# Four cross-attention layers on one Trainium2 core: normalisations and a rotation mask on another engine, scores copied out of PSUM by the instruction that takes their maximum, a fifth share of banks, new ranks

## The chip, the core and the metric

The kernel runs on one core of a Trainium2 chip. A core has a matrix engine (TensorE, PE in the profile, with PEld for its weight loads) and three engines for elementwise work: VectorE (DVE), ScalarE (ACT) and GpSimd (POOL). SyncE (SP) issues the transfers. Matrix products land in PSUM, eight banks of 128 partitions by 512 words; everything else lives in SBUF. Each engine works through its own queue of instructions in order and waits at semaphores for the others. The metric is the device time of one execution in microseconds; the time before is the median of five executions.

## The reference

Sixteen batches of 100 query rows (width 256) pass through four cross-attention layers with 16 heads each, over the same 361 context rows. All is fp32. Cut to what matters:

```python
# L0: heads of 16, layer norm on both sides, then a feed-forward block
qn, kn = layer_norm(x), layer_norm(ctx)
a = softmax(Q(qn) @ K(kn).T / 4); x = x + (a @ V(kn)) @ wo + bo
x = x + gelu(layer_norm(x) @ w1 + b1) @ w2 + b2
# L1: heads of 64, root-mean-square norm on the queries, plain context, no scaling of scores
x = x + (softmax(Q(rms(x)) @ K(ctx).T) @ V(ctx)) @ wo
# L2: heads of 64, rotary embedding on queries and keys, mask over the context
s = rope(Q(x)) @ rope(K(ctx)).T / 8
s = where(mask, s, -1e9)
x = layer_norm(x + (softmax(s) @ V(ctx)) @ Wo) * gamma + beta
# L3: as L0 without the feed-forward block, its own weights
x = x + (softmax(Q(layer_norm(x)) @ K(layer_norm(ctx)).T / 4) @ V(layer_norm(ctx))) @ Wo + bo
```

A softmax here is: the maximum of a row, the exponential of the difference with its sum, a division by the sum.

## The kernel before

**Planned work.** The kernel does not emit instructions as it describes them. `Plan.add` records some 9,000 pieces of work, each with the engines that may do it, a cost, and the buffers that it reads, writes and takes. `Plan.order` (lines 212 to 306) then puts all pieces of all sixteen batches in one order by a simulation of its own: among the pieces whose inputs are done, it takes the one that could start earliest, and among equals the one with the lowest rank. A rank (line 220) is the batch's number times `ORDER["lag"]`, less the length of the chain behind the piece, plus an offset by batch and one for each place in a batch (`ORDER["place"]`, a table of 561 numbers). The same order holds for every engine's queue, so the planner decides what stands behind what. It also chooses between ScalarE and VectorE where a piece names both (copies out of PSUM, biases).

**Tilings.** TensorE works in several tilings: products of the projections and of the weighted values on 32 columns at a time (`col32`), transposes and the scores of heads of 64 on 64 rows (`row64`), the scores of heads of 16 on 32 rows (`row32`). A change of tiling between two pieces costs time; the planner knows it as `Plan.CHANGE` (line 152) and delays such a change by `keep`, `run` and `pull`.

**One unit of attention** (`Attention.unit`, line 817) is four heads. Its scores (L831) take one PSUM bank per head, [100, 361]; `ps_sc`, `SCORE_BANKS = 4` shares, keep the number of banks that hold scores to four of the eight. `exponential` (line 868) then works head by head: in L2 VectorE caps the scores with the mask in place in PSUM (L876); VectorE takes the negated maximum from PSUM (L879); ScalarE reads PSUM and writes the exponential to SBUF with its sum (L882). VectorE inverts the sums of a pair of heads (L854), GpSimd multiplies them in (L861, `divide`), TensorE transposes the pair (L915), ScalarE or VectorE copies the transposes out (L606, L608), and TensorE multiplies with the values (L725). A head's bank is given back when its last reader is done, here the exponential.

**Normalisation.** `inv_root` takes statistics on VectorE (L620 to L627) and a power on GpSimd (L630). `normalize` (L642), the context's three parts (L1271), and L1's scaling (L1286) run on VectorE, from SBUF to SBUF, and TensorE transposes the results (L666, L753). The feed-forward block's result is transposed back to rows at L708 (`rows_of`), from what L1021 adds up.

**Mask.** `make_cap` (L1297) turns the mask bytes into a cap on the scores, on VectorE, for the 100 query partitions. `make_rot` (L1301, L1302) multiplies the rotary tables with the mask bytes on VectorE, so that masked keys become zero. `rotated` (line 769) shuffles pairs on VectorE (L780), multiplies by the sine on GpSimd (L784), by the cosine on VectorE (L787) and adds on GpSimd (L792).

All four layers' instructions pass through the helper lines L606 and L608 (copies), L666, L708, L753, L915 (transposes), L725 (products on columns) and L831 (scores).

Of the kernel before, what the change touches and what calls it, by code (L numbers as in the profile page):

```python
# [19 lines left out]
SK = 361  # L20
# [6 lines left out]
SCORE_BANKS = 4  # L27
# [4 lines left out]
for _name, _w in (  # L32
# [23 lines left out]
    "lag": 78500, "pull": 0.15, "window": 0,  # L56
    "keep": {None: 260, "row64": 220, "row32": 1340, "col64": 2740, "col32": 2110},
    "run": {None: 2810, "row64": 13010, "row32": 14900, "col64": 44290, "col32": 780},
    "batch": (-373500, -1500, 0, 0, 0, 0, 0, 0, 0, 0, 0, 0, 0, 0, -500, -101500),
    "place": [  # L60
        100 * k for k in (
        -195, -25, -956, -1835, -2152, -1031, -1024, -1302, -380, -1684, -1378, -1056, -2143,
        -3503, -2138, -785, -673, -898, 960, -3089, -1622, -888, -1707, -1518, -697, -2594,
        -1339, 95, -552, 834, -1404, -127, -1261, 691, -1769, -3240, -2203, -1157, -1048, 28,
        -1351, -688, -920, -3022, -2221, -2884, -2570, -893, -1744, -2029, -1358, -1963, -574,
        -1155, 17, -756, -2041, -1521, -115, 97, -2134, -4053, -2742, -2111, -2818, -3840,
        -3124, -2876, -1724, -2610, -1441, -3183, -2751, -1243, -1194, -1293, -1145, -686,
        -1119, -1340, -1567, -372, -1031, -924, -2292, -848, 330, 279, 565, -1967, 77, 555, 176,
        -1213, 1890, -682, -1361, -1145, -1613, -2407, -1524, -908, -122, -819, 363, 658, -473,
        671, -312, 275, 803, -56, 224, -1068, -948, 39, -279, 909, 806, 1495, -2344, -641, -365,  # L70
        -2056, 268, 288, 371, -1596, 97, -666, 268, -99, -912, -1342, 664, 971, -162, 644,
        -2607, -1012, -1477, -1806, 110, -1358, -539, -1658, -1535, -477, -899, -135, -1284,
        -619, 912, -401, -85, 320, 1932, 139, -495, -184, 373, -167, -1736, -2576, -440, -217,
        2246, 1243, 167, -139, 817, -1953, -1661, -831, -1697, -332, -1702, -1275, 647, -1595,
        -338, -311, 1148, -1881, -2507, 316, 60, -1823, -8, -1720, -1704, -2198, 50, -2294, 227,
        -718, -333, 1067, 939, 1526, 2811, 212, 1614, -551, 1129, 1032, -489, -2063, 1566, 391,
        952, 203, 611, -129, 132, -78, -1417, -567, 299, 448, 34, -1821, -2597, -2358, -1036,
        -2125, -2751, -2686, -3064, -2566, -4629, -3070, -2280, -1071, -1526, -1652, -1425,
        -1803, -508, -1150, -3650, -1097, -629, -517, 152, -837, -182, -1836, -3200, -737,
        -2498, -1874, 832, -530, -447, -2212, -811, -888, -361, 1315, 84, -1531, 1226, -1587,  # L80
        325, -31, 611, -703, -1882, -102, 203, 100, -832, -220, -996, 1738, 1396, -461, -29,
        -186, 425, 1942, 563, -1378, 733, -6, 2603, 957, 1730, 475, 1401, 1309, 1431, 1393,
        1046, 1305, 985, 1138, 1299, 1081, 573, 1031, 3224, 1048, 1840, 1548, -36, 2079, 1728,
        -1588, -474, -1298, 34, -1814, -781, 1055, 812, 1176, -13, -223, 927, -121, -918, -1891,
        542, -375, 108, 550, -762, -322, 2130, 778, 1512, 1173, 2043, -384, 987, 383, -1008,
        1609, 1373, 1568, 2086, 3318, 3261, 1652, 1329, 652, 1387, 1281, 1633, -27, -308, 884,
        802, 727, -1112, -1621, -2396, -2191, -1331, -1775, 125, 665, -848, -538, 626, -628,
        1211, -537, 607, 1132, 273, -239, 28, 243, 305, -968, -2434, -2636, -2999, -2756, -2813,
        -2412, -2656, -2757, -996, -1431, -1348, -1738, -815, -1208, -2176, -2606, -696, 149,
        1101, -1463, -246, 554, 851, 43, 447, -61, -1392, 1231, 2636, 1100, 200, 331, 1125,  # L90
        1372, 2256, 1020, 986, 332, -1869, -1024, 963, -1748, -457, -2009, -1127, -1766, -3067,
        -2131, -3307, -3273, -4501, -3681, -3221, -2173, -2533, -2964, -5483, -5952, -4641,
        -4415, -2515, -2844, -3131, -3493, -139, 1783, 1636, 111, -1738, -520, -2114, -467,
        -962, 670, -259, -911, 2485, -2308, -501, -251, -2029, 352, -2107, -2183, -1114, 430,
        541, 75, 191, 448, 1236, 131, -2089, -699, -515, -2298, -775, 1387, 926, 2000, 1287,
        1330, 136, -1539, -1198, -419, -1538, -1836, 213, -574, 658, 632, 33, 915, -2280, 1047,
        -440, 1179, 1894, -793, 84, 1260, -1193, -1769, -318, -140, 261, -262, -542, -17, 555,
        -472, -262, 648, -1141, -836, -1855, -208, -131, 359, 1186, 589, 1619, -405, -1818,
        -2228, -556, -264, 755, 859, 1634, 1016, 1947, 706, 874, 137, -104, 716, -1426, -878,
        -1224, -621, -2026, 618, 901, 695, -388, -1702, -260, -2743, -2366, -3079, -1700, -4642,  # L100
        -1450, -1770, -2191, -1929, -1118, -755, -1793, -2871, -5035,
# [48 lines left out]
class Plan:  # L150

    CHANGE = {"row64": 175, "row32": 204, "col64": 172, "col32": 160, None: 190}
# [157 lines left out]
def tile_xattn_layers(  # L310
# [301 lines left out]
    def inv_root(srcs, eps, name, square=False):  # L612
# [4 lines left out]
        def stats(_):  # L617
            for j, (b, f, n) in enumerate(srcs):
                a = mv.ap
                nc.vector.bn_stats(a[:n, j, 2:8], f(b.ap))  # L620
                nc.vector.bn_aggr(a[:n, j, 0:2], a[:n, j, 2:8])
                if square:
                    nc.vector.scalar_tensor_tensor(
                        a[:n, j, 1:2], a[:n, j, 0:1], a[:n, j, 0:1], a[:n, j, 1:2],
                        ALU.mult, ALU.add,
                    )
            nc.vector.tensor_scalar(mv.ap[:, :k, 2], mv.ap[:, :k, 1], eps, None, ALU.add)  # L627

        def power(_):
# [4 lines left out]
        plan.add(  # L634
            on_dve(550, k), stats, reads=[b for b, _, _ in srcs], writes=[mv]
        )
        plan.add(on_pool(550), power, reads=[mv], writes=[mv])
        return mv

    def normalize(mv, dst, src, dst_f, src_f, j, n):  # L640
        def fn(_):
            nc.vector.tensor_scalar(  # L642
                dst_f(dst.ap), src_f(src.ap), mv.ap[:n, j, 0:1], mv.ap[:n, j, 3:4],
                ALU.subtract, ALU.mult,
            )

        plan.add(on_dve(E), fn, reads=[mv, src], writes=[dst])
# [4 lines left out]
    def queries_T(src, p, name, cls="xT", affine=None):  # L652
# [20 lines left out]
        for i, (q0, q1) in enumerate(parts):  # L673
# [6 lines left out]
            for c in range(2):  # L680

                def scaled(eng, i=i, c=c, q0=q0, q1=q1):
# [8 lines left out]
                    on_act(q1 - q0 + 100) + on_dve(q1 - q0 + 60), scaled,  # L691
# [107 lines left out]
    class Attention:  # L799
# [17 lines left out]
        def unit(self, i):  # L817
# [9 lines left out]
            def scores(_):  # L827
# [11 lines left out]
                on_pe((half, 4 * len(groups))), scores, reads=[self.q, *keys],  # L839
# [28 lines left out]
        def exponential(self, bank, share, sums, j, h, probs):  # L868
            neg_max = plan.buf("two", f"mx_{self.name}_{h}")
            prob = probs[h] = plan.buf("prob", f"prob_{self.name}_{h}")  # L870

            def s():
                return bank.ap[:S, :SK]
# [512 lines left out]
```

## Time and profile before

| what | value |
|---|---|
| median of 5 executions | 1969.51 us (1965.54 to 1971.88) |
| the profiled execution's own time | 1965.42 us |
| its span | 1963.5 us |
| granted TensorE clock, mean | 0.995 |
| TensorE busy with matmuls | 1914.3 us, 97% |
| GpSimd: divide (L861), 1024 instructions | 576.7 us, 579 ns each |
| ScalarE: exponential (L882), 1024 | 566.7 us, 565 ns each, and 204 ns each to read the accumulator |
| VectorE: normalisation of rows (L642), 48 | 38.4 us, 800 ns each |
| VectorE: normalisation of the context (L1271), 48 | 31.0 us, 651 ns each |
| VectorE: rotation mask (L1301 and L1302), 16 each | 931 and 1581 ns each |

How to read it: a line of a group names the source line, the engine, the operation, what it writes and reads with shapes, the count, the busy time and the mean of one in ns, and behind the bar the idle time of that engine just before these instructions and who ended it. In the timeline a line begins with its start and its length in us. A line of the waits reads "who waited for whom: us in total, times, longest". Matmuls are pipelined, so their lengths overlap; the distance from one start to the next tells more.

### The profile page before, as it was taken

How to read it: one execution, taken by the hardware profiler on the slowest of the kernel's cores; microseconds unless marked ns; L12 is line 12 of the kernel's file. 1: busy time of each engine (PE TensorE's matmuls, PEld its weight loads, DVE VectorE, ACT ScalarE, POOL GpSimd, SP SyncE). 2: the span in 40 equal slices, each digit the busy share in tenths (PEclk: the TensorE clock that was granted, in tenths of full speed). 3: DMA queues.
4: the chain of work that ended last, by engine and by line, in shares of the span. 5: the costliest groups of instructions: out<-in, count | busy, mean ns of one | idle time of the engine just before them, and what ended most of it. 6: DMA issues, size and time to landing. Idle time of an engine off the chain costs nothing.

```text
span 1963.5 us, 99209 instructions
## 1 busy us (share of the span) xinstructions
PE 1914.3 (97%) x43881; PEld 1266.9 (65%) x43881; DVE 1387.9 (71%) x3802; ACT 1134.2 (58%) x3398; POOL 958.0 (49%) x1522
## 2 busy tenths in 40 slices
PE   8999999999999999999999999999999999999997
PEld 4766575666766657666576666757566676665765
DVE  5656777767777677777767777677776777766676
ACT  4545555565556656566565665655556555664645
POOL 4354545544455453545445455454554445544544
PEclk9999999999999999999999999999999999999998
DMA  7000000000000000000000000000000000000000
GB/s 300 3 3 14 5 12 7 3 14 5 14 5 3 14 5 14 6 11 6 5 14 5 12 8 3 14 5 12 7 4 14 5 14 5 4 14 5 3 3 7
DMA packets 14726, 29.91 MB, mean 15 GB/s; under 512 B 3362, under 2 KB 12376, under 8 KB 12888
## 3 DMA queue, kind: packets, MB, share of 16 engines
q1 hardware_dynamic: 14296, 23.56, 3.7%
q8 instruction: 345, 5.65, 1.2%
q14 instruction: 85, 0.70, 0.1%
HBM read 21.92 MB, written 1.64 MB: 12 GB/s over the span
## 4 chain that ended last, share of the span: by engine, by line
PE 82%; DVE 11%; POOL 3%; issue 1%; ACT 1%; DMA 1%; SPq 0%; ACTq 0%; POOLq 0%; DVEq 0%
PE ps L725 58%; PE ps L831 12%; PE ps L915 10%; POOL prob L861 2%; DVE two L879 2%; DVE ps L876 1%; DVE rot L1302 1%; POOL sw L784 1%; DVE mv L620 1%; DVE ctxr L1271 1%; DMA slab<-slabs_dram 1%; PE ps L666 1%; DVE sw L780 1%; ACT prob L882 1%; DVE z L642 1%
## 5 line engine op out<-in xcount | busy, mean ns | idle before, releaser
L861 POOL TENSOR_SCALAR prob<-prob,two 100x361 f32<-100x361 f32 x1024 | 576.7, 579 | 729.7 <-DVE two L854 693.7
L882 ACT ACTIVATE prob<-ps,two 100x361 f32<-100x361 f32 x1024 | 566.7, 565 | 288.8 <-DVE two L879 260.9
L879 DVE TENSOR_REDUCE two<-ps 100x1 f32<-100x361 f32 x1024 | 486.4, 524 | 163.5 <-PE ps L831 162.2
L725 PE MATMUL ps<-slab,cT 128*32 128x512 f32 (+1 forms) x3072 | 363.4, 595 | 0.8 <-DMA slab<-slabs_dram 0.8
L725 PE MATMUL ps<-cT,slab 128*32 128x361 f32 x4096 | 357.0, 468 | 1.5 <-DMA slab<-slabs_dram 1.2
L831 PE MATMUL ps<-kT,qT 32*100 32x181 f32 (+3 forms) x4096 | 301.0, 328 | 0.3 <-DVE qT L1087 0.3
L606 ACT COPY pT<-ps 128x384 f32<-128x384 f32 (+1 forms) x522 | 232.2, 497 | 96.0 <-PE ps L915 63.5
L831 PEld LDWEIGHTS ps<-kT,qT 32*100 32x100 f32 (+1 forms) x4096 | 229.8, 165 | 77.1 <-issue 38.9
L915 PEld LDWEIGHTS ps<-ident,prob 64*128 64x128 f32 (+1 forms) x6144 | 214.6, 139 | 89.8 <-POOL prob L861 43.7
L915 PE MATMUL ps<-ident,prob 64*128 64x64 f32 (+1 forms) x6144 | 238.5, 226 | 11.7 <-POOL prob L861 11.6
L882 ACT ACTIVATION_READ_ACCUMULATOR prob<-ps,two 100x1 f32 x1024 | 208.9, 204 | 0.0
L725 PEld LDWEIGHTS ps<-cT,slab 128*32 128x32 f32 x4096 | 123.9, 109 | 116.4 <-issue 101.8
L725 PEld LDWEIGHTS ps<-slab,cT 128*32 128x32 f32 (+1 forms) x3072 | 88.1, 108 | 152.0 <-issue 136.4
L608 DVE COPY pT<-ps 128x384 f32<-128x384 f32 (+1 forms) x246 | 134.1, 570 | 63.8 <-PE ps L915 51.2
L784 POOL TENSOR_TENSOR sw<-sw,rot 128x361 f32<-128x361 f32 x128 | 105.6, 826 | 141.0 <-PE ps L725 66.7
L606 ACT COPY v<-ps 105x512 f32<-105x512 f32 (+1 forms) x145 | 84.9, 586 | 144.6 <-PE ps L725 144.5
L725 PE MATMUL ps<-pT,v 128*32 128x100 f32 (+1 forms) x6144 | 160.1, 251 | 2.1 <-DVE pT L608 1.2
L725 PEld LDWEIGHTS ps<-pT,v 128*32 128x32 f32 (+1 forms) x6144 | 138.4, 110 | 36.0 <-issue 27.2
L876 DVE TENSOR_TENSOR ps<-ps,cap 100x361 f32<-100x361 f32 x256 | 125.0, 532 | 22.5 <-PE ps L831 21.7
L725 PEld LDWEIGHTS ps<-xT,slab 128*32 128x32 f32 x5120 | 115.0, 111 | 20.5 <-issue 15.4
L725 PE MATMUL ps<-xT,slab 128*32 128x100 f32 x5120 | 125.2, 251 | 1.8 <-issue 1.4
L792 POOL TENSOR_TENSOR kT<-kT,sw 128x361 f32<-128x361 f32 x128 | 122.3, 957 | 3.9
(101 smaller groups left out, 2152.0 us busy)
## 6 DMA issues: line engine op xcount, KB each, us to landing
slab<-slabs_dram SPq DMA_DIRECT2D x11, 1024.0 KB
ctxr<-ctx_dram SPq DMA_DIRECT2D x16, 256.0 KB
ctxr<-ctx_dram SPq DMA_DIRECT2D x16, 105.0 KB
x<-x_dram SPq DMA_DIRECT2D x16, 100.0 KB
out_dram<-x SPq DMA_DIRECT2D x16, 100.0 KB
slab<-slabs_dram SPq DMA_DIRECT2D x2, 512.0 KB
mask<-mask_dram SPq DMA_DIRECT2D x16, 45.1 KB
rows<-rowvecs_dram SPq DMA_DIRECT2D x1, 640.0 KB
```

The source lines that it names most:

```text
L606: nc.scalar.copy(dst(), src())
L608: nc.vector.tensor_copy(dst(), src())
L620: nc.vector.bn_stats(a[:n, j, 2:8], f(b.ap))
L725: nc.tensor.matmul(out_f(at + t, at + t1), lhsT=lhsT[:, t:t1], rhs=rhs, start=start, stop=stop, tile_position=(0, at + t),)
L784: nc.gpsimd.tensor_tensor(a, a, wide(sin()), ALU.mult)
L792: nc.gpsimd.tensor_tensor(dst_f(dst.ap), dst_f(dst.ap), sw.ap[:, :n], ALU.add)
L831: nc.tensor.matmul(banks[h].ap[:S, k0:k1], lhsT=self.q_of(h), rhs=self.k_of(h)[:, k0:k1], start=(k0 == 0), stop=(k1 == SK), skip_group_che ...
L861: nc.gpsimd.tensor_scalar(p.ap[:S, :SK], p.ap[:S, :SK], rsum.ap[:S, j : j + 1], 1.0, ALU.mult, ALU.mult,)
L876: nc.vector.tensor_tensor(s(), s(), self.cap.ap[:S, :], ALU.min)
L879: nc.vector.tensor_reduce(neg_max.ap[:S, 0:1], s(), AX.X, ALU.max, negate=True)
L882: nc.scalar.activation(prob.ap[:S, :SK], s(), AF.Exp, bias=neg_max.ap[:S, 0:1], accum_out=sums.ap[:S, j : j + 1],)
L915: nc.tensor.transpose(out[:, c, :], probs[h].ap[q0:q1, c * KP : (c + 1) * KP], ident[q0:q1, q0:q1],)
```

## The change

The change moves work between engines, changes what frees a bank of scores, and sets new constants for the planner:

- `normalize` runs on GpSimd, as (x + (-mean)) x root; `inv_root` negates the mean for it, in one more VectorE instruction. The context's three parts and L1's scaling go the same way.
- The rotation mask is made on GpSimd, by clipping the cap to 0..1 and multiplying the two tables with that; the cap is now made on all 128 partitions.
- Unmasked heads (L0, L1, L3): one VectorE instruction reads the scores from PSUM, writes their negatives to SBUF and accumulates the minimum, which is the negated maximum; the exponential then reads SBUF with scale -1. Masked heads (L2): the cap's minimum is written to SBUF, and maximum and exponential read it there. The bank and its share are given back after VectorE's reading.
- Five shares for banks of scores in place of four; other costs for a number of pieces; other `CHANGE` values; another `ORDER`.

```diff
-SCORE_BANKS = 4
+SCORE_BANKS = 5
 ORDER = {
-    "lag": 78500, "pull": 0.15, "window": 0,
-    "keep": {None: 260, "row64": 220, "row32": 1340, "col64": 2740, "col32": 2110},
-    "run": {None: 2810, "row64": 13010, "row32": 14900, "col64": 44290, "col32": 780},
-    "batch": (-373500, -1500, 0, 0, 0, 0, 0, 0, 0, 0, 0, 0, 0, 0, -500, -101500),
+    "lag": 262500, "pull": 1.05, "window": 0,
+    "keep": {None: 4710, "row64": 360, "row32": 180, "col64": 5940, "col32": 2180},
+    "run": {None: 0, "row64": 28190, "row32": 38220, "col64": 62800, "col32": 390},
+    "batch": (-548000, -33500, 0, 0, 0, 0, 0, 0, 0, 0, 0, 0, 0, 0, 14000, -395500),
...
-    CHANGE = {"row64": 175, "row32": 204, "col64": 172, "col32": 160, None: 190}
+    CHANGE = {"row64": 170, "row32": 191, "col32": 141, None: 190}
...
             nc.vector.tensor_scalar(mv.ap[:, :k, 2], mv.ap[:, :k, 1], eps, None, ALU.add)
+            nc.vector.tensor_scalar(mv.ap[:, :k, 4], mv.ap[:, :k, 0], -1.0, None, ALU.mult)
...
     def normalize(mv, dst, src, dst_f, src_f, j, n):
         def fn(_):
-            nc.vector.tensor_scalar(
-                dst_f(dst.ap), src_f(src.ap), mv.ap[:n, j, 0:1], mv.ap[:n, j, 3:4],
-                ALU.subtract, ALU.mult,
+            nc.gpsimd.tensor_scalar(
+                dst_f(dst.ap), src_f(src.ap), mv.ap[:n, j, 4:5], mv.ap[:n, j, 3:4],
+                ALU.add, ALU.mult,
             )
-        plan.add(on_dve(E), fn, reads=[mv, src], writes=[dst])
+        plan.add(on_pool(395), fn, reads=[mv, src], writes=[dst])
...
             def mask_off(_):
-                nc.vector.tensor_tensor(s(), s(), self.cap.ap[:S, :], ALU.min)
+                nc.vector.tensor_tensor(p(), bank.ap[:S, :SK], self.cap.ap[:S, :], ALU.min)
             def maximum(_):
-                nc.vector.tensor_reduce(neg_max.ap[:S, 0:1], s(), AX.X, ALU.max, negate=True)
+                nc.vector.tensor_reduce(neg_max.ap[:S, 0:1], p(), AX.X, ALU.max, negate=True)
+            def negated(_):
+                nc.vector.tensor_scalar(
+                    p(), bank.ap[:S, :SK], -1.0, None, ALU.mult, ALU.min,
+                    accum_out=neg_max.ap[:S, 0:1],
+                )
             def exp(_):
                 nc.scalar.activation(
-                    prob.ap[:S, :SK], s(), AF.Exp, bias=neg_max.ap[:S, 0:1],
+                    p(), p(), AF.Exp, bias=neg_max.ap[:S, 0:1], scale=1.0 if masked else -1.0,
                     accum_out=sums.ap[:S, j : j + 1],
                 )
-            if self.cap is not None:
-                plan.add(on_dve(SK), mask_off, reads=[bank, self.cap], writes=[bank])
-            plan.add(on_dve(SK), maximum, reads=[bank], writes=[neg_max])
+            if masked:
+                plan.add(on_dve(SK), mask_off, reads=[bank, share, self.cap], writes=[prob])
+                plan.add(on_dve(SK), maximum, reads=[prob], writes=[neg_max])
+            else:
+                plan.add(on_dve(SK + 70), negated, reads=[bank, share], writes=[prob, neg_max])
             plan.add(
-                [("ACT", 538.0, 660.0)], exp, reads=[bank, share, neg_max], writes=[prob, sums]
+                [("ACT", 538.0, 660.0)], exp, reads=[prob, neg_max], writes=[prob, sums]
             )
...
-            nc.vector.tensor_scalar(z.ap, xt.ap, mv.ap[:S, 0, 3:4], None, ALU.mult)
+            nc.gpsimd.tensor_scalar(z.ap, xt.ap, mv.ap[:S, 0, 3:4], 1.0, ALU.mult, ALU.mult)
...
         def make_rot(_):
-            nc.vector.tensor_tensor(rot.ap[:, 0, :], cos_k, mu.ap, ALU.mult)
-            nc.vector.tensor_tensor(rot.ap[:, 1, :], sin_k, mu.ap, ALU.mult)
+            on = rot.ap[:, 0, :]
+            nc.gpsimd.tensor_scalar(on, cap.ap, 1.0, 0.0, ALU.min, ALU.max)
+            nc.gpsimd.tensor_tensor(rot.ap[:, 1, :], sin_k, on, ALU.mult)
+            nc.gpsimd.tensor_tensor(on, cos_k, on, ALU.mult)
```

The table `ORDER["place"]` is new throughout.

## The prediction

> **What bounds the kernel now.** I read the busy shares first, then the chain of work that ended last, then the groups, and last the waits and the timeline around the places where TensorE stood still. All durations are of the one profiled execution (span 1963.5 us, its time 1965.4 us).
>
> ```profile
> PE 1914.3 (97%) x43881; PEld 1266.9 (65%) x43881; DVE 1387.9 (71%) x3802; ACT 1134.2 (58%) x3398; POOL 958.0 (49%) x1522
> PE 82%; DVE 11%; POOL 3%; issue 1%; ACT 1%; DMA 1%; SPq 0%; ACTq 0%; POOLq 0%; DVEq 0%
> ```
>
> TensorE is the bound, and the change leaves its 43,881 matmuls as they are. So the time can only change by what stands between the matmuls: changes of the array's tiling, and waits. I measured both as the distance from the first matmul of one planned piece (1,973 in all) to the first of the next, and took the median of a piece followed by one of its own tiling as its price.
>
> ```profile
> 1050.53 1.05 PE L725 MATMUL ps<-slab,oT 128*32 128x256 f32 x16
> 1051.51 0.59 PE L753 MATMUL ps<-ident,ctxr 64*128 64x64 f32 x12
> ...
> 1052.77 1.06 PE L725 MATMUL ps<-slab,zT 128*32 128x256 f32 x16
> 1053.66 1.89 PE L725 MATMUL ps<-slab,cT 128*32 128x512 f32 x16
> ```
>
> Sixteen matmuls of one size take 0.98 us before transposes (another tiling; 1050.53 to 1051.51) and 0.89 before a piece of their own. Medians over all records: such a piece 863 ns and 977; the wide value piece 1717 and 1831; key projection 1214 and 1328; transposes 372 and 491. A tiling change costs 93 to 119 ns. The account closes: first matmul at 6.0, pieces 1795.2, 752 tiling changes 81.0, 94 waits over 100 ns 63.3, jitter 13.0, which makes 1958.4, where the last piece starts; 5.1 us follow.
>
> Of the 63.3, 11.0 lie in the first 100 us (weights, folding) and 21.5 in the last 60 (two batches left, little to fill in). In the middle the order repeats with each batch, and 26 us are three places, 14 times each: 0.64 us ahead of the transposes of L0's normalised rows, 0.51 ahead of those of the feed-forward result, and right after it 0.70 ahead of L2's probabilities (1.86 per batch). The waits name their releasers, some 14 to 16 times each where the place has the line for itself:
>
> ```profile
> PEld ps L708 <- ACT prob L882: 14.5, 14, 1.1
> PEld ps L666 <- DVE z L642: 13.5, 16, 1.6
> ```
>
> And the timeline shows why they are late:
>
> ```profile
> 1054.09 1.18 DVE L1271 TENSOR_SCALAR ctxr<-ctxr,mv 128x256 f32<-128x256 f32 x1
> ...
> 1056.01 1.11 DVE L642 TENSOR_SCALAR z<-x,mv 100x256 f32<-100x256 f32 x1
> ...
> 1057.17 0.33 PE L666 MATMUL ps<-ident,z 64*128 64x64 f32 x4 [0.58 <-DVE z L642]
> ```
>
> ```profile
> 1105.77 1.82 DVE L1302 TENSOR_TENSOR rot<-cst,mask 128x361 f32<-128x361 f32 x1 [1.79 <-POOL sw L784]
> ...
> 1107.51 0.97 DVE L876 TENSOR_TENSOR ps<-ps,cap 100x361 f32<-100x361 f32 x2
> ...
> 1112.24 2.20 POOL L861 TENSOR_SCALAR prob<-prob,two 100x361 f32<-100x361 f32 x4 [4.21 <-DVE two L854]
> ...
> 1112.55 0.32 PE L708 MATMUL ps<-ident,rT 64*100 64x64 f32 x4 [0.45 <-ACT prob L882]
> ```
>
> Normalisations and the rotation mask run on VectorE from SBUF to SBUF while GpSimd is at work there too, and take two to three times what such a shape costs elsewhere:
>
> ```profile
> L642 DVE TENSOR_SCALAR z<-x,mv 100x256 f32<-100x256 f32 x48 | 38.4, 800 | 26.3 <-POOL mv L630 26.3
> L1302 DVE TENSOR_TENSOR rot<-cst,mask 128x361 f32<-128x361 f32 x16 | 25.3, 1581 | 23.3 <-POOL sw L784 23.3
> L1313 DVE TENSOR_SCALAR x<-x,mv 100x256 f32<-100x256 f32 x16 | 7.0, 435 | 9.4 <-POOL mv L630 9.4
> L879 DVE TENSOR_REDUCE two<-ps 100x1 f32<-100x361 f32 x1024 | 486.4, 524 | 163.5 <-PE ps L831 162.2
> ```
>
> **The change part by part.**
>
> *Normalisations and rotation mask to GpSimd.* VectorE loses 48 x 800 + 48 x 651 (L1271) + 16 x 345 (L1286) + 16 x (931 + 1581) = 115 us and gains 96 negations at 172 (L627) = 16.5. GpSimd gains 112 one-input instructions; the divide, 361 wide, takes 579 (L861), by proportion 411 at 256, and the one 256-wide row 497 (L536), so I take 0.45 each, 50 us, and 16 masks of one one-input and two two-input instructions (579 + 2 x 826, L784) = 36 us: 958 becomes 1044, 53%. The first place (0.64) loses the two slow instructions of the timeline; the chain gets a negation of 0.17 and loses 0.35 of normalisation and a hop between engines. The third place (0.70) loses the 1.82 us ahead of L876. What may now be late is the normalisation itself, queued on GpSimd behind up to four divides (2.2 us, as at 1112.24).
>
> The Trainium skill speaks against this part: its GPSIMD Engine Reference, section "Engine selection", sends elementwise work to VectorE and calls GpSimd about twice as slow with two inputs. The rows here say the opposite for this place: VectorE took 800 and 1581 where GpSimd takes 579 and 826. By the rule this part would lose time on the chain; by the rows it takes away the waits above.
>
> *Scores leave PSUM with their maximum.* For 768 unmasked heads a TENSOR_SCALAR with an accumulated minimum takes the place of a 524 ns reduce. No row shows VectorE accumulating. Lower end: 524, since a plain PSUM copy of this width takes 529 (L608) and no row is faster. Upper end: 587 (L1052, same shape, PSUM to SBUF) plus 204, what ScalarE pays to read its accumulator (L882), together 791. I take 590, by L1052, the nearest row: VectorE then stands at 1388 - 115 + 16 + 51 = 1340 us, 68%. Hidden: the exponentials of a pair come every 0.65 us, so only the first maximum of four shows, +0.07 us per unit. At 791 the cover is gone, since VectorE then sets the pace.
>
> The skill's VectorE: DVE Perf Modes, section "Two Vector instructions with no wait between them", counts an operation that writes out its accumulator as two instructions. It gives no price; by it one would lean to the upper end.
>
> The 256 masked heads keep two instructions; a minimum from PSUM into SBUF (523, L787) is no dearer than in place (532), the reduce then reads SBUF. ScalarE's exponential now reads SBUF; no ScalarE row does. On VectorE SBUF and PSUM sources differ little (426 at L1316, 418 at L998); I take 565 as before, with 100 ns to either side (464 to 572 is what ScalarE's 361-wide rows span), hidden at 58% load. The gain: a bank comes free after VectorE's pass and not after the exponential. That is the second place (0.51, released by L882).
>
> *Five banks of scores, new ranks.* A unit needs four shares, so a fifth lets the next scores start when one head is still held. The ranks change the order itself. I counted in the built programs: tiling changes go from 752 to 844, six more per batch; with the prices above 81.0 becomes 90.9, **+10 us**, on the path, with nothing to hide it. For it the order buys room. For each of the 32 pairs of heads in a batch I compared the PE work between its scores and its transposes with the time that its softmax took in the trace of before (scores' end to last divide). Before, the median margin is 1.3 us, nine pairs have under 0.5, and two (L2's heads 8 to 11) are at -1.3: the third place. In the new order the median is 2.3, one is at -0.1 (L2's heads 4 and 5, whose 12.1 us was mostly queueing), and the two at -1.3 have 5.4 and 6.1.
>
> *New tight places*, per batch: L2's rotated queries have 5.0 us of PE work before their scores (11.8 before) for a chain of 2.7 (shuffle 0.58 and GpSimd 1.04 twice) that can meet four divides (2.2); the copy of the last weighted values before an output projection has 0.69 (1.22 before) for about 0.6; the feed-forward's rows to L1's transposes have 3.3 for a chain that took 3.3. I put 0.1 to 0.15 on each, 0.43 x 14 = **+6 us**; ends 0 and 21 (half a microsecond on each).
>
> *Sum.* -26 (three places) + 10 (tiling changes) + 6 = -10 us; start and end, whose sequence of pieces is nearly the old one, at 0 (ends 4 to either side). 1965.4 becomes 1955.4. The profiled execution lies 4.1 us below the median of the runs (1969.5), so on that footing 1959.5.
>
> **Rivals.**
> 1. *More is gained*: the new order's room also covers the tight places, and start and end give 4: -26 + 10 - 4 = -20, 1949.5. For it: the wider margins. Against: rooms of 0.69 and 5.0.
> 2. *The wait moves to GpSimd*: normalisations stand behind divides, as the divides of before stood behind each other, and half a microsecond at two more places is 14 us less of the gain: about +4, 1970 to 1973; no measurable change. For it: GpSimd's blocks of four divides. Against: 53% load.
> 3. *Slower: the accumulating pass is dear.* At 791 VectorE carries +205 us instead of +51 and needs 0.8 us more per unit of four heads. The point where it decides is the smallest ordinary margin of the new order, 0.52 us over four heads (L3's first pairs), that is 130 ns a head, a pass of 650 or more. At 791 four pairs per batch with margins of 0.5 to 0.9 and the adds behind them lose about 1.5 us: +21, in all -26 + 10 + 6 + 21 = +11, 1980.5.
> 4. *The order doesn't do what it says*: the six extra tiling changes are certain, the gain isn't; without any of the three places gone, +10 to +16. Held within 2 and 3, since the causes at two places are removed by the first part alone.
>
> **How the numbers follow.** Forecast 0.43, rival 1 0.21, rival 2 0.15, rival 3 (and 4) 0.21. A measurement of this kernel can tell some 0.2%, 4 us, from no change. Faster 0.64, same 0.14, slower 0.22. The range runs from rival 1 with the lower end of its terms (1946) to where the upper end of the new waits leaves the forecast and most of rival 2, and the first half of rival 3 (1976).
>
> **What would show it.** No waits of TensorE for a normalisation on VectorE (now L666's) or for an exponential (now L708's); the accumulating pass near 590; normalisations near 0.45 on GpSimd; about 844 tiling changes; PE's sum of waits in the middle near 0.5 us per batch. It is wrong if the pass takes over 650, if transposes wait for GpSimd at new places for more than a microsecond per batch, or if the last 60 us lose more than before.

## The result, and the profile after

The changed kernel takes 1970.15 us (median of 26 executions, 1965.13 to 1972.6), the kernel before 1968.18 us in the same comparison (47 executions, 1965.11 to 1972.73). The ratio is 1.0007, 95% interval 1.0002 to 1.0012: no change that matters, where a gain of 10 us was forecast. The time lies inside the predicted range and on the wrong side of the forecast.

The busy shares and the engines' shares of the chain that ended last, from the page of the kernel after (span 1966.3 us):

```profile
PE 1923.1 (98%) x43881; PEld 1267.4 (64%) x43881; DVE 1275.7 (65%) x4452; ACT 1196.6 (61%) x3470; POOL 1043.3 (53%) x1680
...
PE 89%; ACT 3%; POOL 3%; DVE 2%; issue 1%; DMA 0%; SPq 0%; DVEq 0%; POOLq 0%; ACTq 0%
```

VectorE's share of the chain fell from 11% to 2%, as wanted, and ScalarE's rose from 1% to 3%. PE's share rose from 82% to 89%, and the time did not fall: a chain that is more TensorE is no shorter by itself. The account of the prediction (distance from the first matmul of a piece to that of the next), made again for this trace, says where the time is. All in us; "middle" leaves out the first 100 us and the last 60:

| | before | after | difference |
|---|---|---|---|
| first matmul | 6.0 | 5.3 | -0.6 |
| pieces at their own price | 1795.2 | 1795.2 | 0 |
| tiling changes | 81.0 (752) | 90.9 (844) | +9.9 |
| waits over 100 ns | 63.3 (94) | 57.7 (83) | -5.6 |
| of these, in the middle | 30.8 | 31.0 | +0.2 |
| jitter | 13.0 | 12.1 | -0.9 |
| start of the last piece | 1958.4 | 1961.3 | +2.9 |

The differences sum to the 2.8 us by which the spans differ, within rounding. The three old places of the middle are gone, some 25 us by this account. But the middle's waits add up to 31.0 again, and one new place holds 16.0 of them: 1.45 us (1451 to 1455 ns) in each of 11 batches (those numbered 3 to 13, of 0 to 15), ahead of L1's query projection. In the batches outside these 11 another piece stands ahead of the projection, and it does not wait. The next largest are the transposes of L2's probabilities (7.5 us in ten waits of 0.1 to 1.6) and L0's normalised rows, which now follow another piece (13 waits of 0.2, 2.9 us). The waits of TensorE's weight loads, and the first line of the waits of its matmuls, name who ends the new one (kernel after; "who waited for whom: us in total, times, longest"):

```profile
PEld ps L926 <- POOL prob L862: 50.6, 79, 1.0
...
PEld ps L726 <- ACT xT L607: 23.7, 11, 2.2
```

```profile
PE ps L726 <- ACT xT L607: 13.7, 11, 1.2
```

The upper line is the larger total, spread over 79 short waits of a weight load that mostly runs ahead under the matmuls, so only a part of it reaches them. The next one is eleven waits of some 2.2 us, released by ScalarE's copy of `xT`, and the matmuls themselves wait for the same copy eleven times. That regularity, more than the total, marks a wait that repeats with the batch. The timeline around it, kernel after (start, length, engine, line, operation; in brackets the idle time ahead and who ended it):

```profile
995.37 0.27 ACT L607 COPY x<-ps 100x128 f32<-100x128 f32 x1 [4.49 <-PE ps L709]
...
998.44 0.33 PE L667 MATMUL ps<-ident,z 64*128 64x64 f32 x4
...
998.71 1.92 PE L726 MATMUL ps<-slab,cT 128*32 128x512 f32 x16
998.88 0.22 ACT L607 COPY xT<-ps 128x72 f32<-128x72 f32 x1 [1.85 <-PE ps L667]
999.12 1.28 ACT L891 ACT_TABLE_LOAD   x1
...
1000.41 0.60 ACT L891 ACTIVATE prob<-prob,two 100x361 f32<-100x361 f32 x1
...
1001.00 0.58 ACT L891 ACTIVATE prob<-prob,two 100x361 f32<-100x361 f32 x1
...
1001.58 0.24 ACT L607 COPY xT<-ps 128x128 f32<-128x128 f32 x1
...
1001.88 2.35 PE L726 MATMUL ps<-xT,slab 128*32 128x100 f32 x100 [1.25 <-ACT xT L607]
```

TensorE transposes L1's scaled rows (998.44), does one wide value piece meanwhile (998.71) and then needs both copies of the transposed rows. The first copy follows at once (998.88). The second stands in ScalarE's queue behind two exponentials of L2, and ahead of those ScalarE loads the table of the exponential, 1.28 us. From 998.71 to 1001.88 are 3.17 us for a piece whose price is 1.72: the difference is the 1.45. The first line shows the other half of it: just before, ScalarE stood idle for 4.49 us. It had run the feed-forward's GELU (L1257, until 990.9), and the table for the next exponential is loaded where that exponential stands in the queue and not where there is time. The planner books both table loads in GELU's own cost (`8 * 245 + 2560`), so in its simulation this place is not tight.

The operations that the prediction had to guess, in the groups of the kernel after:

```profile
L891 ACT ACTIVATE prob<-prob,two 100x361 f32<-100x361 f32 x1024 | 604.8, 595 | 141.5 <-DVE prob L885 101.9
L885 DVE TENSOR_SCALAR_CACHE_REDUCE prob<-ps 100x361 f32<-100x361 f32 x768 | 375.2, 529 | 80.1 <-PE ps L832 62.0
```

The accumulating pass takes 529 ns, and a second instruction that reads the accumulator 83 (768 times, 63.4 us in all): 612, where 590 was taken. The exponential from SBUF takes 595, where 565 was taken.

### The profile page after: what moved, and what is told of

It reads as the page before. It is cut to its first block, busy times and chain, and to the rows that moved or that the text cites. A ratio compares the mean times of both kernels' runs of the same rounds, so it can differ in the third digit from the quotient of the medians.

```text
span 1966.3 us, 99772 instructions
## 1 busy us (share of the span) xinstructions
PE 1923.1 (98%) x43881; PEld 1267.4 (64%) x43881; DVE 1275.7 (65%) x4452; ACT 1196.6 (61%) x3470; POOL 1043.3 (53%) x1680
## 4 chain that ended last, share of the span: by engine, by line
PE 89%; ACT 3%; POOL 3%; DVE 2%; issue 1%; DMA 0%; SPq 0%; DVEq 0%; POOLq 0%; ACTq 0%
PE ps L726 64%; PE ps L832 14%; PE ps L926 10%; ACT prob L891 2%; POOL prob L862 1%; DVE prob L885 1%; PE ps L667 1%; ACT L891 1%; DVE pT L609 1%; POOL kT L793 1%; PE ps L754 0%; POOL sw L785 0%; PE ps L709 0%; POOL mv L632 0%; POOL z L643 0%
## 5 line engine op out<-in xcount | busy, mean ns | idle before, releaser
L862 POOL TENSOR_SCALAR prob<-prob,two 100x361 f32<-100x361 f32 x1024 | 568.2, 570 | 477.5 <-DVE two L855 389.6
L891 ACT ACTIVATE prob<-prob,two 100x361 f32<-100x361 f32 x1024 | 604.8, 595 | 141.5 <-DVE prob L885 101.9
L885 DVE TENSOR_SCALAR_CACHE_REDUCE prob<-ps 100x361 f32<-100x361 f32 x768 | 375.2, 529 | 80.1 <-PE ps L832 62.0
L726 PE MATMUL ps<-cT,slab 128*32 128x361 f32 x4096 | 348.0, 469 | 2.3 <-DMA slab<-slabs_dram 1.6
L926 PEld LDWEIGHTS ps<-ident,prob 36*128 36x128 f32 (+1 forms) x6144 | 217.9, 140 | 86.9 <-POOL prob L862 50.6
L609 DVE COPY pT<-ps 128x432 f32<-128x432 f32 (+1 forms) x228 | 126.0, 578 | 129.7 <-PE ps L926 129.1
L891 ACT ACTIVATION_READ_ACCUMULATOR prob<-prob,two 100x1 f32 x1024 | 196.1, 192 | 0.0
L607 ACT COPY v<-ps 128x512 f32<-128x512 f32 (+1 forms) x136 | 79.3, 583 | 166.0 <-PE ps L726 166.0
L879 DVE TENSOR_TENSOR prob<-ps,cap 100x361 f32<-100x361 f32 x256 | 126.5, 525 | 32.2 <-PE ps L832 28.1
L855 DVE RECIPROCAL two<-two 100x2 f32<-100x2 f32 x512 | 81.5, 160 | 94.8 <-ACT prob L891 93.4
```

Source lines behind the costliest of these rows:

```text
L607: nc.scalar.copy(dst(), src())
L609: nc.vector.tensor_copy(dst(), src())
L726: nc.tensor.matmul(out_f(at + t, at + t1), lhsT=lhsT[:, t:t1], rhs=rhs, start=start, stop=stop, tile_position=(0, at + t),)
L855: nc.vector.reciprocal(rsum.ap[:S], sums.ap[:S])
L862: nc.gpsimd.tensor_scalar(p.ap[:S, :SK], p.ap[:S, :SK], rsum.ap[:S, j : j + 1], 1.0, ALU.mult, ALU.mult,)
L879: nc.vector.tensor_tensor(p(), bank.ap[:S, :SK], self.cap.ap[:S, :], ALU.min)
```

## The experiments

Twelve kernels, in three groups; each ratio is to the kernel before in the same comparison (1968.6, 1966.65 and 1966.12 us). "Place" numbers are waits of TensorE per batch in us, and "middle" the sum of the middle's waits, both from the account above.

### What is the 1.45, and what would the change be worth without it?

Theory 1: the second copy's position behind the table load and the exponentials. Theory 2: the tiling changes and the new order's lack of room, of which this wait is only the sign. Two kernels take the wait away in two ways that have nothing in common, a third does both, and a fourth gives the kernel before the same early table.

**e1_copy_ahead**: the copies of L1's transposed rows go right behind their transposes in the finished order.

```diff
-        for work in plan.order():
+        works = plan.order()
+        for b in range(B):
+            at = next(i for i, k in enumerate(works) if k.engine == "PE" and k.bufs[-1].name == f"L1_xT_{b}_ps1")
+            copies = [k for k in works if k.engine != "PE" and k.bufs[0].name.startswith(f"L1_xT_{b}_ps")]
+            works = [k for k in works if k not in copies]
+            works[at + 1 : at + 1] = copies
+        for work in works:
```

> The changed kernel with one edit in the finished order: the copies of L1's transposed rows stand right behind their transposes in ScalarE's queue, ahead of two exponentials of L2 (and of the table load that comes with the first); all else keeps its place. Theory 1 (one new wait ate the gain: TensorE stands 1.45 us before L1's queries in every batch, since the second copy is queued behind a table load of 1.28 us and two exponentials): the wait goes, 14 x 1.45 = 20 us less, some 1946 to 1950 against 1966 in the profile; L2's exponentials come 0.25 us later, which may cost 1 to 3 us. Theory 2 (the 92 added changes of tiling are what ate it, and waits only move about): under 5 us of gain.

Measured: 1951.9 us, ratio 0.9918 (0.9904 to 0.9931). The place goes from 1.45 to 0.02, the middle from 31.0 to 13.6. ScalarE and TensorE in e1_copy_ahead, at the same point of the same batch:

```profile
993.13 0.39 ACT L607 COPY xT<-ps 128x72 f32<-128x72 f32 x2 [1.85 <-PE ps L667]
993.53 1.28 ACT L891 ACT_TABLE_LOAD   x1
994.70 1.55 PE L726 MATMUL ps<-xT,slab 128*32 128x100 f32 x63
```

Both copies now stand ahead of the load, and the projection follows the wide value piece at once (994.70). By the ratios 17.5 us went, less than the 20 expected: that sum took the place for 14 waits, and it has 11.

**e2_table_early**: an exponential of one column, whose result nobody reads, behind the GELU loop, so that ScalarE loads the table there.

```diff
+    spare = const.tile([P, 1], F32, name="spare")
...
+            nc.scalar.activation(spare[:, 0:1], neg_half[:, 0:1], AF.Exp)
```

> The changed kernel with a one-column exponential right behind the GELU, whose result nobody reads, so that ScalarE loads the table of the exponential while it has nothing to do; the planner's order is untouched. Theory 1a (the table load is what makes the copy late): the copy comes up to 1.28 us earlier, the wait of 1.45 shrinks to about 0.2 to 0.6 (the exponentials still wait for VectorE's maxima, ready at 999.3 in the profile, and for each other), 12 to 17 us less. Theory 1b (the two exponentials and VectorE's maxima make it late, the table load hides beside the maxima): under 5 us less. Theory 2 (changes of tiling): no gain.

Measured: 1949.69 us, ratio 0.9904 (0.9889 to 0.9919). The place falls to 0.04, the middle to 11.4. The timeline of ScalarE in e2_table_early, at the same point of the same batch:

```profile
982.54 1.99 ACT L1258 ACTIVATE qT<-ps,colt 128x100 f32<-128x100 f32 x8
984.55 1.28 ACT L1262 ACT_TABLE_LOAD   x1
985.85 0.20 ACT L1262 ACTIVATE spare<-neg_half 128x1 f32<-128x1 f32 x1
...
992.64 0.60 ACT L892 ACTIVATE prob<-prob,two 100x361 f32<-100x361 f32 x1
...
993.24 0.58 ACT L892 ACTIVATE prob<-prob,two 100x361 f32<-100x361 f32 x1
...
993.82 0.25 ACT L608 COPY xT<-ps 128x128 f32<-128x128 f32 x1
```

And TensorE there:

```profile
992.09 0.33 PE L668 MATMUL ps<-ident,z 64*128 64x64 f32 x4
992.36 1.92 PE L727 MATMUL ps<-slab,cT 128*32 128x512 f32 x16
994.11 1.13 PE L727 MATMUL ps<-xT,slab 128*32 128x100 f32 x41
```

The load lies at 984.55, in time that ScalarE had free. The second copy still stands behind the two exponentials, and ends at 994.07. The wide value piece is followed after 1.75 us instead of 3.17.

**e3_both**: the two edits together.

> Both edits of the two runs before in the changed kernel. Theory 1: the copy's wait is gone by the first edit already; the early table adds room for L2's last probabilities (waits of up to 1.6 us at the transposes of L2's last pairs in some batches), so 20 to 26 us less than the changed kernel, 1940 to 1946 in the profile. Theory 2: under 5 us less.

Measured: 1949.1 us, ratio 0.9901 (0.9887 to 0.9916); middle 9.5. It is not to be told from e2_table_early, since one edit had already emptied the place.

**e4_before_table_early**: the one-column exponential of e2 in the kernel before.

> The kernel before with the same one-column exponential behind the GELU. The prediction put the wait of 0.70 us before L2's probabilities down to the slow rotation mask on VectorE, and the 0.51 before it to a bank that the exponential holds. If that is all, the early table changes little (under 4 us). If the table load of 1.28 us at the first exponential after the GELU was part of both chains, both waits shrink or go, and the time falls by 0.5 to 1.2 us per batch, 7 to 17 us, without anything else of the change.

Measured: 1964.54 us, ratio 0.9982 (0.9973 to 0.9991). The place at L2's probabilities stays at 0.70, the one at the feed-forward's rows goes from 0.51 to 0.34: of the two outcomes named, the first (under 4 us).

What follows: theory 1 holds. Twice, in two ways, this one wait went while the 844 tiling changes kept their cost, and the time fell by 17.5 and 20.3 us by the ratios. 16.0 of that is the wait itself; the early table also took most of what the transposes of L2's probabilities waited (7.5 us in the changed kernel, 1.2 with it). Without the wait the change is a gain of 16 to 19 us on the kernel before (0.8 to 1.0%), near rival 1's size. The early table alone is worth 0.2% (3.5 us) on the kernel before, so most of the gain is not the table's.

### Is it the engine, or the room in the order?

Theory A: the moved work gains because GpSimd does it without disturbance. Theory B: the new order left room, and the engine matters little. First with the new order held fixed, from e2_table_early; then in the old order, part by part.

**e5_norm_on_vector**: e2_table_early with all normalisations on VectorE again and no negated mean.

```diff
-            nc.gpsimd.tensor_scalar(
-                dst_f(dst.ap), src_f(src.ap), mv.ap[:n, j, 4:5], mv.ap[:n, j, 3:4],
-                ALU.add, ALU.mult,
+            nc.vector.tensor_scalar(
+                dst_f(dst.ap), src_f(src.ap), mv.ap[:n, j, 0:1], mv.ap[:n, j, 3:4],
+                ALU.subtract, ALU.mult,
```

> The changed kernel with the early table, and the normalisations and L1's scaling back on VectorE at their places in the same finished order (no negation of the mean). Theory A (the move to GpSimd is what took away the wait of 0.64 us before L0's normalised rows): normalisations cost 650 to 800 ns again, waits of some 0.4 to 0.7 us come back at L0's, L3's or the feed-forward's normalised rows, 5 to 12 us slower than with the early table alone (1949.7), so about 1955 to 1962. Theory B (the new order's room took the waits away, whatever the engine): within 4 us of 1949.7.

Measured: 1949.4 us, ratio 0.9912 (0.9898 to 0.9926), middle 11.3 against 11.4. Its group:

```profile
L643 DVE TENSOR_SCALAR z<-x,mv 100x256 f32<-100x256 f32 x48 | 21.1, 440 | 2.5 <-POOL mv L632 2.4
```

The same instruction took 800 ns on VectorE in the kernel before. Here it takes 440, less than GpSimd's 570 in the kernel after. So "slow on VectorE" is no property of the instruction alone. The context's parts, on the same line of the same kernel, did not get faster (651 ns in the kernel before):

```profile
L643 DVE TENSOR_SCALAR ctxr<-ctxr,mv 128x256 f32<-128x256 f32 (+1 forms) x48 | 32.7, 703 | 0.3 <-POOL mv L632 0.3
```

The single instructions of the kernel before show what goes with the slow ones. Of its 48 normalisations of rows, the 18 that ran beside a divide of GpSimd or beside an idle GpSimd took 0.41 us on average, the 29 that ran beside GpSimd's two-input addition of the rotary embedding (L792) 1.05. Of the context's parts in e5_norm_on_vector, the 27 beside that addition took 0.94, the 19 beside an idle GpSimd 0.40. The neighbour alone does not settle it: 13 rows of e5_norm_on_vector overlapped the addition and still took 0.40.

The sum stayed the same, but two small waits changed places: the 0.2 ahead of L0's normalised rows is gone, and one of 0.2 came in 11 batches ahead of L1's query projection.

**e6_mask_on_vector**: e2_table_early with the mask's three instructions (`nc.gpsimd` to `nc.vector` in `make_rot`) on VectorE.

> The changed kernel with the early table, and the three instructions of the rotation mask on VectorE at their places in the same order. Theory A (the mask on VectorE is what made L2's first probabilities late): 0.3 to 0.7 us per batch come back at the transposes of L2, 4 to 10 us slower than 1949.7. Theory B (the order's room: L2's heads 8 to 11 have 5.4 and 6.1 us to spare now): within 3 us of 1949.7.

Measured: 1949.01 us, ratio 0.9907 (0.9893 to 0.9920), middle 10.0. The three instructions take 505, 688 and 752 ns on VectorE, against 492, 823 and 826 on GpSimd in the kernel after. With the new order, both engine moves are worth nothing that can be measured: theory B.

**e7_before_norm_on_gpsimd**: the kernel before, with the reverse edit of e5 (normalisations to GpSimd, the negated mean added).

> The kernel before in its own order, with the normalisations, the context's and L1's scaling on GpSimd (as the change does it, negation included). Theory A: the 0.64 us before L0's rows go or shrink to under 0.2; 7 to 9 us less than before, about 1960, unless GpSimd's divides hold them up. Theory B: GpSimd's queue makes the rows or L2's rotated keys later than VectorE did: no gain or a loss of up to 10 us.

Measured: 1978.08 us, ratio 1.0058 (1.0045 to 1.0072), some 11 us more: theory B. The place ahead of L0's rows, which this edit was to remove, grows from 0.64 to 0.75, and new ones of 0.32 (ahead of L1's values, for a late copy of the context), 0.19 and 0.16 come. The timeline of GpSimd and TensorE in e7_before_norm_on_gpsimd shows the first:

```profile
1063.51 0.55 POOL L631 TENSOR_TENSOR mv<-mv,neg_half 128x1 f32<-128x1 f32 x1
...
1064.06 0.55 POOL L1272 TENSOR_SCALAR ctxr<-ctxr,mv 128x256 f32<-128x256 f32 x1
...
1064.57 0.82 POOL L785 TENSOR_TENSOR sw<-sw,rot 128x361 f32<-128x361 f32 x1
...
1065.38 0.56 POOL L643 TENSOR_SCALAR z<-x,mv 100x256 f32<-100x256 f32 x1
...
1065.99 0.33 PE L667 MATMUL ps<-ident,z 64*128 64x64 f32 x4 [0.68 <-POOL z L643]
```

The rows' root is ready at 1064.06, and the rows are normalised at 1065.38: a part of the context and a multiplication of the rotary embedding stand between them in GpSimd's queue, as parts of the context stood ahead of them in VectorE's. In this order the delay moved with the work to the other engine. That does not clear VectorE's slow instruction in the kernel before: there the normalisation took 1.11 us (at 1056.01), 0.70 more than the 0.41 of an undisturbed one, and the wait was 0.64.

**e8_before_mask_on_gpsimd**: the kernel before, with the mask on GpSimd.

```diff
-            nc.vector.tensor_tensor(rot.ap[:, 0, :], cos_k, mu.ap, ALU.mult)
-            nc.vector.tensor_tensor(rot.ap[:, 1, :], sin_k, mu.ap, ALU.mult)
+            on = rot.ap[:, 0, :]
+            nc.gpsimd.tensor_scalar(on, mu.ap, 1.0, 0.0, ALU.min, ALU.max)
+            nc.gpsimd.tensor_tensor(rot.ap[:, 1, :], sin_k, on, ALU.mult)
+            nc.gpsimd.tensor_tensor(on, cos_k, on, ALU.mult)
```

> The kernel before in its own order, with the rotation mask made on GpSimd (from the mask bytes; in the planned place, which is ahead of L2's rotated keys and between divides). Theory A: VectorE reaches L2's cap 1.8 us sooner, the 0.70 us before L2's probabilities go and part of the 0.51 before them, 8 to 15 us less than before. Theory B (GpSimd's 2.1 us stand in front of the divides that TensorE waits for): the wait stays or grows by up to 1.4 us per batch, 0 to 20 us more.

Measured: 1955.18 us, ratio 0.9940 (0.9927 to 0.9952). The places of 0.70 and 0.51 are both gone; one of 0.39 comes at L1's transposes. In this group of e8_before_mask_on_gpsimd the idle time of ScalarE ahead of the table loads of the exponential is 17.8 us:

```profile
L882 ACT ACT_TABLE_LOAD x16 | 20.5, 1283 | 17.8 <-DVE two L879 17.8
```

In the kernel before:

```profile
L882 ACT ACT_TABLE_LOAD x16 | 20.5, 1283 | 47.6 <-DVE two L879 47.6
```

Here theory A is right: in the old order the mask's 2.5 us on VectorE stood ahead of L2's maxima, and ScalarE's load waited with the exponential behind them.

### The new maximum and the new ranks, by themselves

**e9_before_new_maximum**: the old order, with the new way out of PSUM (negatives with accumulated minimum, exponential from SBUF) for the 1,019 of 1,024 heads whose place in SBUF is free by then. The rest keep the old way, and the bank stays held by the planner's order until after the exponential.

> The kernel before in its own order, with the change's way out of PSUM for 1019 of the 1024 heads (five, whose buffer for probabilities is not free yet at that place of the order, keep the old way). Theory A (the earlier release of a bank is what it brings): the wait of 0.51 us before the feed-forward's rows, released by an exponential, goes; the other two stay: 7 us less, about 1960. Theory B (a pass of 612 us with its accumulator's reading in place of 524 makes VectorE later): the 0.70 and 0.64 grow, 0 to 10 us more.

Measured: 1973.71 us, ratio 1.0041 (1.0027 to 1.0054). The place at L2's probabilities grows from 0.70 to 0.87, that at the feed-forward's rows is 0.46 for 0.51, and new ones of 0.16 to 0.26 come: theory B. The exponential no longer ends the wait ahead of the feed-forward's rows; VectorE's addition that makes them (L1037) does, late in the queue behind the mask and the maxima. The old order gains nothing from a bank that is free earlier, and pays the longer passes.

**e10_old_maximum**: e2_table_early with the old way (maximum from PSUM, exponential from PSUM) for the 902 heads whose bank is not taken again ahead of their exponential. In both kernels a list of heads picks the path:

```diff
-                    p(), p(), AF.Exp, bias=neg_max.ap[:S, 0:1], scale=1.0 if masked else -1.0,
+                    p(), out(), AF.Exp, bias=neg_max.ap[:S, 0:1],
+                    scale=1.0 if masked or prob.name not in plan.new else -1.0,
```

> The changed kernel with the early table, in its own order, with the old way for the 902 heads whose bank is not taken again ahead of the exponential: the maximum by a reduce from PSUM, the exponential from PSUM (masked heads capped in place). Theory A (the new order needs the banks early): TensorE waits for banks at exponentials, 5 to 20 us slower than 1949.7. Theory B (room enough, and VectorE has 88 ns less per head): within 4 us of 1949.7.

Measured: 1993.36 us, ratio 1.0141 (1.0125 to 1.0158), some 44 us above e2_table_early. The middle goes from 11.4 to 47.7, and TensorE's weight loads wait for exponentials again (e10_old_maximum):

```profile
PEld ps L834 <- ACT prob L901: 29.5, 50, 1.3
...
PEld ps L728 <- ACT prob L901: 19.3, 61, 1.0
```

L834 are the scores, which wait for a bank. Theory A is right here, and its size was expected far too small (5 to 20 us): the new order needs the early release of banks.

**e11_before_new_ranks**: the work and the four shares of the kernel before, planned with the new `ORDER` and the new `CHANGE`.

> The kernel before with the change's ranks and costs of tiling alone (four shares, all work as before); the planner makes another order with 877 changes of tiling. The 125 more cost 13 to 14 us by the prices of the accounts. Theory A (ranks alone bring the room): waits in the middle shrink by more than that, 1950 to 1965. Theory B (ranks fit only the work that they were made for): waits stay or grow, 1980 to 2000.

Measured: 2139.96 us, ratio 1.0878 (1.0849 to 1.0908): 877 tiling changes (95.4 us), and some 170 us of waits between its first 100 us and its last 60. Theory B, and far beyond its range: on the old work, with four shares, the new ranks are a loss.

**e12_before_three_parts**: the old order with the mask on GpSimd (e8), the new maximum (e9) and the early table (e2).

> The kernel before in its own order, with the mask on GpSimd, the new way out of PSUM (1019 heads) and the early table, but the normalisations on VectorE. If the parts add up as measured alone (mask -11.5, early table -4, new way 0 to -7, less what they share), 1946 to 1955: as fast as the changed order with its one wait taken out, with 92 fewer changes of tiling. If the order has no room for the longer VectorE pass, 1957 to 1965.

Measured: 1959.32 us, ratio 0.9965 (0.9952 to 0.9978). By their ratios the three edits gave -11.8, +8.1 and -3.5 us each by itself, -7.2 together; measured are -6.9. In the old order these parts add up, to the second of the two outcomes named, and end 10 to 12 us short of the new order with the early table. The 0.63 ahead of L0's rows is still there, and so is the one at L1's transposes that came with the mask's move (0.38).

Not tried: the changed work with the old ranks, and with four shares (the planner finds no order for them).

## Why the prediction was wrong, point by point

- **The three places, -26 us**: about right in size (the trace of before has 13, 14 and 13 such waits in the middle, some 25 us). All three are gone in the kernel after; a wait of 0.2 us ahead of L0's rows, behind another piece, is new. Of the reasons given, one is shown. The third (0.70) was the mask on VectorE, as e8_before_mask_on_gpsimd shows. The second (0.51) was put down to banks; it went with the mask too, and e9_before_new_maximum left it at 0.46 with another releaser, so the bank's early release alone does not remove it. For the first (0.64) the prediction blamed VectorE's two slow instructions; e7_before_norm_on_gpsimd took them off VectorE and the place grew, so the move is no cure in the old order. Whether they were the cause there stays open: the slow instruction cost 0.70 us, as much as the wait. In the new order the same work on VectorE costs nothing (e5_norm_on_vector), so the gain is not the engine's.
- **The tiling changes, +10 us**: right. 844 changes cost 90.9 us at the prices of the kernel before, which still fit (a wide value piece ahead of another tiling takes 1831 ns in both kernels).
- **The new tight places, +6 us: this is the step that failed.** The prediction put "0.1 to 0.15 on each" of three places, with half a microsecond as its upper end. The third was "the feed-forward's rows to L1's transposes have 3.3 for a chain that took 3.3". The chain was the right one and was followed one link too short: the wait falls behind those transposes, at the copy that the query projection needs, and is 1.45 us in 11 batches, 16.0 us in all, where 0.15 in 14 would have made 2. At the other two places the middle shows no wait over 0.1 us; 7.5 us came at L2's last transposes instead, 2.9 at L0's rows, and some 5 elsewhere. The middle's 31.0 us stand against 12: the 6 of the sum and some 6 of other waits in the kernel before. The sum's upper end of 21 would have made 27. In the new order the load, two exponentials and the copy come in one row, 1.28 + 0.60 + 0.58 us after the first copy, against 1.72 of TensorE's work. The prediction compared rooms for the softmax of every pair and for rows, but did not list what stands in ScalarE's queue ahead of each copy that TensorE waits for, and it counted no table load. The chain's length was taken from before, where the table load came 7 us ahead of these copies, and the two copies followed each other:

```profile
1109.45 1.28 ACT L882 ACT_TABLE_LOAD   x1 [3.44 <-DVE two L879]
...
1116.68 0.39 ACT L606 COPY xT<-ps 128x72 f32<-128x72 f32 x2 [0.93 <-PE ps L666]
```

- **What the step was worth**: with 2 us in place of the 16.0 the time of 1970.2 would have been near 1956, inside the range and below the kernel before; e1_copy_ahead, which leaves nothing of the place and a little less elsewhere, measured 1951.9.
- **The accumulating pass** (rival 3): 612 against 590, under the 650 from which it was to decide. The rival falls.
- **The exponential from SBUF**: 595 against 565, within the 100 given and hidden, as forecast.
- **The normalisation on GpSimd**: 570 for 100 x 256 against 450, and hidden but for the 0.2 us ahead of L0's rows. VectorE stands at 1276 us (forecast 1340). About half of the difference is that the planner gave 72 more of the copies and biases to ScalarE (33 us less on VectorE); GpSimd stands at 1043 (1044).
- **Rival 2** foresaw the shape, a wait that takes the place of those removed, with about the right end (1970 to 1973), but on GpSimd. GpSimd's part is the 2.9 us ahead of L0's rows; the large new wait came from ScalarE's queue.
- **Start and end**, put at 0, gained: the last 60 us lose 16 against 21.5 of before, and with the first matmul and the jitter some 7 us went. That was not foreseen, and it is luck that it hid part of the miss: without it the changed kernel would have been slower by about 10 us. Of the signs named in advance, the waits of the middle spoke: 31.0 us, 2.2 per batch, not 0.5; the pass, the normalisations' hiding and the count of changes did not.

What is shown: the wait, its cause, and its worth (two edits, each of which takes it away). Shown too is that the new order needs the early release of banks (e10), that the old order gains nothing from it (e9), and that the new ranks lose on the old work (e11). What stays open is how much each rank and the fifth share contribute, and what made L0's first place in the kernel before.

## What to carry to other kernels

When an order is replaced, follow each chain that TensorE waits on through to the copy that it really needs, and list everything that stands ahead of that copy in its engine's queue, table loads included: the load of ScalarE's table comes where the next other function stands, not where the plan books it. Switching the table back in idle time, by a one-column instruction of 0.2 us, gave back 20 us here, and 3.5 in the kernel before. Within one order the parts can add up, as in e12_before_three_parts; an order and its work do not come apart so easily: constants tuned for one set of work cost 174 us on another. And an instruction that is "slow on its engine" may be slow only beside its neighbours: look at its single instances before moving it, since another order may do as much as another engine.

## What the runs showed of the hardware

- A table load of ScalarE took 1283 ns in every kernel, and is held back with the instruction that needs it: in the kernel before it stood behind 47.6 us of waiting in 16 loads, though ScalarE was free. Placed behind the GELU, it ran at once (e2_table_early, 0.3 us of idle time ahead of 16 loads).
- One VectorE instruction that copies 100 x 361 out of PSUM, negates and accumulates a minimum took 529 ns, the same as a plain copy of that width (529 in the kernel before), plus 83 ns to read the accumulator; ScalarE's reading takes 192 to 204.
- ScalarE's exponential took 595 ns from SBUF (kernel after) and 565 from PSUM (kernel before); in e10_old_maximum, which has both, 604 and 568.
- VectorE's normalisation of 100 x 256 from SBUF to SBUF took 800 ns on average in one order and 440 in another, the same instruction with the same data. In the first, it took 0.41 us beside a divide of GpSimd or beside an idle GpSimd (18 times) and 1.05 beside GpSimd's two-input addition L792 (29 times).
